# Six tiles for the broadcasts of B and C, three for the weight pieces, five for the convolutions' results, in a decoder layer on one core

## The chip, the cores and the metric

The kernel runs on one core of one Trainium2 chip. The core has five engines that run side by side: PE (matrix products), DVE (vector work), ACT (activation functions and copies), POOL (here small fills and copies, and the DMAs with indices) and SP, which only issues DMAs. Each takes its instructions in its own fixed order and waits at semaphores for the others. On-chip memory (SBUF) has 128 partitions; PE writes into a small second memory (PSUM).

The metric is the device time of one execution in microseconds. The kernel before takes 5619.11 us, the median of three runs (5616.44 to 5622.24).

## What is computed

Input x is 8 x 512 x 512, with a context of the same size. Three parts follow each other, each added to its input and normalised over the last axis (all float32):

```python
x = _layernorm(x + mamba(x))              # L0_attn: state-space layer
x = _layernorm(x + cross_attn(x, ctx))    # L0_xattn: 16 heads of 32, softmax over 512 keys
x = _layernorm(x + moe(x))                # L0_ffn: 32 experts, 4 per token, and a shared one
```

The first part is what the change is in:

```python
xn = layernorm(x) * ln_w + ln_b
x_main, z = split(xn @ in_proj_w, 2)                 # 1024 channels each
x_main = silu(causal_conv(x_main, conv_w) + conv_b)  # 4 taps, per channel
dt, B, C = split(x_main @ x_proj_w, [32, 48])        # 32 | 16 states | 16 states
dt = softplus(dt @ dt_proj_w + dt_proj_b)
h_t = exp(A * dt_t) * h_{t-1} + dt_t * B_t * x_t     # per channel and state
y_t = sum_n h_t * C_t
out = res_scale * ((y + x_main * D) * silu(z)) @ out_proj_w + x
```

The mixture of experts picks 4 of 32 experts per token (first 4 of 8 groups by their best score, then the 4 best scores), gives each expert 640 places, and sends every token's row to its places; the gate's small comparisons are touched by the change too.

## The kernel before

Three functions run after each other: `layers` (state-space layer, attention, gate and shared expert, for all batches), `experts` and `finish` (the last normalisation). All of the change is in `layers`.

`layers` goes through 16 chunks: 8 batches b, each in two halves t of T = 256 tokens. A chunk has 32 steps k = 0 to 31: four channel pairs q, in each four groups g of four states, in each two channel blocks (L980, L1032). A step is, in this order: copy the state into h (`carry`, on ACT), four exponentials for the next step's decays (`decays`, L437, ACT), then on DVE the product of dt*x and B (L449) and the scan over 256 tokens (L453), then the product with C (L470), and on PE the sum over states into `py` (L474). The tile h has four buffers, the decays two.

Beside the steps run, at fixed k, the parts of the same and of neighbouring chunks:

- k = 1, 2: `back`, the out-projection of the chunk before (L503), then its norm and the store to x1d;
- k = 3 to 6: `gate_x`, the z half of the in-projection (L305);
- k % 8 = 3: `prepare` of the next channel pair: dt by one small matmul, on ACT Abs, Relu, Exp, Ln (L406, tile `l`) and Identity (L408), on DVE four operations (L412 to L415; `l` is read last at L414), and eight loads that lay dt and dt*x out as `both` (L426);
- k = 5, 9, 11: load, norm and transpose of the next chunk's x;
- k = 12, 15, 18, 21: `convolve` for the next chunk: in-projection (L305), POOL puts the tail of the last chunk in front (L322, L324), ACT copies PSUM behind it (L325, tile `xp`) and makes the first tap (L331, tile `xs`), DVE adds three taps (L339);
- k = 23, 24: silu and `x_proj` for the next chunk, whose B and C go to DRAM (`scr`).

Side work, the attention, gate and shared expert of batch b - 1, is a list of units with weights, strewn over the steps (L1080); the last batch's runs alone at the end of `layers` (L1102). Then `experts` begins.

Three kinds of loads matter here, all issued by SP (L381, L265, L426). `bcast` (L374) loads the next group's two tiles, B and C, each in two halves, broadcast over 64 partitions: 128 KB written per load, four loads per two steps, from the pool `l_bc` of four tiles. `pieces` (L246) yields the in- and out-projection's weights in pieces of 512 KB, always asked for one piece ahead, in two buffers of the tile `wm`. The convolutions' results `xs` live from the convolution to the end of their channel pair in the next chunk, in six buffers.

A tile pool gives each tag its number of buffers; a new tile of a tag takes the buffer of the oldest and must wait for its last reader. The program text is not the order of issue: a planner in the framework orders each engine's instructions at build time by readiness as it estimates it and by program order, and may draw an instruction far ahead when its inputs and a free buffer are there. On the chip the order is then fixed.

Of the kernel before, what the change touches and what calls it, by code (L numbers as in the profile page):

```python
# [7 lines left out]
F32 = mybir.dt.float32  # L8
# [8 lines left out]
P = 128  # L17
B, S, D = 8, 512, 512
# [8 lines left out]
T = 256  # L27
# [7 lines left out]
SC = S // P  # L35

E = 32
K = 4
G = 8
# [3 lines left out]
CAP = int(1.25 * N * K / E)  # L43
SLOTS = E * CAP
# [37 lines left out]
def layers(ctx, tc, a, x1d, filld, based, xbuf):  # L82
# [23 lines left out]
    nc = tc.nc  # L106
    cp = ctx.enter_context(tc.tile_pool(name="l_const", bufs=1))
    sm = ctx.enter_context(tc.tile_pool(name="l_small", bufs=2))
    gm = ctx.enter_context(tc.tile_pool(name="l_gate", bufs=1))
    p1 = ctx.enter_context(tc.tile_pool(name="l_p1", bufs=1))  # L110
    p2 = ctx.enter_context(tc.tile_pool(name="l_p2", bufs=2))
    p3 = ctx.enter_context(tc.tile_pool(name="l_p3", bufs=2))
    bcp = ctx.enter_context(tc.tile_pool(name="l_bc", bufs=4))
    dp = ctx.enter_context(tc.tile_pool(name="l_dram", bufs=2, space=DRAM))
    psm = ctx.enter_context(tc.tile_pool(name="l_psm", bufs=2, space=PSUM))
    psy = ctx.enter_context(tc.tile_pool(name="l_psy", bufs=1, space=PSUM))
# [14 lines left out]
    def rows(w):  # L131
        return w.rearrange("(c p) f -> p c f", p=P)
# [29 lines left out]
    for da in das:  # L162
# [21 lines left out]
        pattern=[[1, G], [-1, G]],  # L184
        compare_op=ALU.is_gt,
        fill=0.0,
        base=0,
        channel_multiplier=0,
    )

    early = cp.tile([P, SC, E], F32, name="l_early")
    nc.gpsimd.iota(
        early, pattern=[[0, SC], [-1, E]], base=E, channel_multiplier=0, allow_small_or_imprecise_dtypes=True
    )
    first = cp.tile([P, SC, E], F32, name="l_first")
    nc.gpsimd.iota(
        first, pattern=[[0, SC], [CAP, E]], base=-SLOTS, channel_multiplier=0, allow_small_or_imprecise_dtypes=True
    )

    taken = cp.tile([P, SC + 1, E], F32, name="l_taken")  # L200
    nc.gpsimd.memset(taken, 0.0)
# [44 lines left out]
    def pieces():  # L246


        w_in, w_out = rows(a["in_proj_w"]), rows(a["out_proj_w"])
        xs = [w_in[:, :, 2 * q * P : 2 * (q + 1) * P] for q in range(CC // 2)]  # L250
        zs = [w_in[:, :, DI + 2 * q * P : DI + 2 * (q + 1) * P] for q in range(CC // 2)]
        outs = [w_out[:, 2 * q : 2 * q + 2, :] for q in range(CC // 2)]
        n = B * (S // T)
        order = list(xs)
        for i in range(n):
            order += (outs if i else []) + zs + (xs if i + 1 < n else [])
        order += outs
        got = None
        for src in order + [None]:
            nxt = None  # L260
            if src is not None:
                nxt = p2.tile([P, 4 * 2 * P], F32, tag="wm", name="wm").rearrange(
                    "p (c f) -> p c f", c=src.shape[1]
                )
                nc.sync.dma_start(nxt, src)  # L265
            if got is not None:
                yield got
            got = nxt

    piece = pieces()  # L270

    def load_x(b, t, f):
# [27 lines left out]
    def project(f, name):  # L300
        w = next(piece)
        ps = psm.tile([P, 2, T], F32, tag="mm", name=name)
        for i in range(2):
            for dc in range(DC):
                nc.tensor.matmul(  # L305
                    ps[:, i, :],
                    w[:, dc, i * P : (i + 1) * P],
                    f["xnT"][:, dc, :],
                    start=(dc == 0),
                    stop=(dc == DC - 1),  # L310
                )
        return ps

    def convolve(t, q, f):

        c0 = 2 * q
        ps = project(f, "ps_x")

        def first_tap():
            xp = p1.tile([P, 2, T + 3], F32, tag="xp", name="xp")  # L320
            if t == 0:
                nc.gpsimd.memset(xp[:, :, 0:3], 0.0)  # L322
            else:
                nc.gpsimd.tensor_copy(xp[:, :, 0:3], conv_tail[:, c0 : c0 + 2, :])  # L324
            nc.scalar.copy(xp[:, :, 3:], ps)  # L325
            if t < S // T - 1:
                nc.gpsimd.tensor_copy(conv_tail[:, c0 : c0 + 2, :], xp[:, :, T : T + 3])
            f["xs"][q] = xs = p2.tile([P, 2, T], F32, tag="xs", name="xs", bufs=6)
            for i in range(2):
                c = c0 + i  # L330
                nc.scalar.activation(  # L331
                    xs[:, i, :], xp[:, i, 0:T], AF.Identity, bias=cb[:, c : c + 1], scale=cw[:, c, 0:1]
                )

            def other_taps():
                for i in range(2):
                    acc = xs[:, i, :]
                    for k in range(1, 4):
                        nc.vector.scalar_tensor_tensor(  # L339
                            acc, xp[:, i, k : k + T], cw[:, c0 + i, k : k + 1], acc, ALU.mult, ALU.add  # L340
                        )

            return other_taps

        return first_tap
# [28 lines left out]
    def bcast(f, g):  # L374

        got = []
        for r0 in (g * NG, NST + g * NG):
            t = bcp.tile([P, NG // 2, T], F32, tag="bc", name="bc")
            for r in range(2):
                n0 = r0 + r * NG // 2  # L380
                nc.sync.dma_start(  # L381
                    t[r * HP : (r + 1) * HP], f["scr"][n0 : n0 + NG // 2, :].partition_broadcast(HP)
                )
            got.append(t.unsqueeze(1).to_broadcast([P, 2, NG // 2, T]))
        return got

    def prepare(q, f):

        ps = psm.tile([P, 2, T], F32, tag="mm", name="ps_dt")
        for i in range(2):  # L390
            c = 2 * q + i
            nc.tensor.matmul(
                ps[:, i, :], w_dt[:, c * P : (c + 1) * P], f["xd"][0:RANK, :], start=True, stop=True
            )

        def exponentials():
            u = p1.tile([P, 2, T], F32, tag="u", name="u")
            dt = p1.tile([P, 2, T], F32, tag="dt", name="dt")

            for i in range(2):  # L400
                c = 2 * q + i
                nc.scalar.activation(u[:, i, :], ps[:, i, :], AF.Abs, bias=b_dt[:, c : c + 1])
                nc.scalar.activation(dt[:, i, :], ps[:, i, :], AF.Relu, bias=b_dt[:, c : c + 1])
            nc.scalar.activation(u, u, AF.Exp, scale=-1.0)
            l = p1.tile([P, 2, T], F32, tag="l", name="l")
            nc.scalar.activation(l, u, AF.Ln, bias=1.0)  # L406
            w = dtx = p1.tile([P, 2, T], F32, tag="dtx", name="dtx")
            nc.scalar.activation(w, u, AF.Identity, bias=1.0)  # L408

            def both():  # L410

                nc.vector.scalar_tensor_tensor(w, w, -1.0, u, ALU.add, ALU.subtract)  # L412
                nc.vector.tensor_tensor(l, l, w, ALU.subtract)
                nc.vector.tensor_tensor(dt, dt, l, ALU.add)  # L414
                nc.vector.tensor_tensor(dtx, dt, f["xs"][q], ALU.mult)  # L415
                for i in range(2):
                    c = 2 * q + i
                    nc.scalar.activation(
                        f["xs"][q][:, i, :], f["xs"][q][:, i, :], AF.Identity, scale=dpar[:, c : c + 1]
                    )  # L420
                f["ready", q] = []
                for src in (dt, dtx):
                    to = p2.tile([P, 2, 2, T], F32, tag=f"both{len(f['ready', q])}", name="both")
                    for r in range(2):
                        for j in range(2):
                            nc.sync.dma_start(to[r * HP : (r + 1) * HP, :, j, :], src[j * HP : (j + 1) * HP])  # L426
                    f["ready", q].append(to)

            return both

        return exponentials
# [7 lines left out]
    def carry(t, c, g):  # L439

        last = state[:, c, g].unsqueeze(2)
        h = p3.tile([P, NG, T + 1], F32, tag="h", name="h", bufs=4)
        nc.scalar.copy(h[:, :, 0:1], last if t else nothing)  # L443
        return h
# [99 lines left out]
    def choose(b, x2t, pl, st):  # L544
# [13 lines left out]
        square = [P, SC, G, G]  # L558
        other = gs.unsqueeze(2).to_broadcast(square)
        own = gs.unsqueeze(3).to_broadcast(square)  # L560
        eq = gm.tile(square, F32, tag="g_eq", name="g_eq")
        nc.vector.tensor_tensor(eq, other, own, ALU.is_equal)
        nc.vector.tensor_tensor(eq, eq, lower.unsqueeze(1).to_broadcast(square), ALU.mult)
        gt = gm.tile(square, F32, tag="g_gt", name="g_gt")
        nc.vector.tensor_tensor(gt, other, own, ALU.is_gt)
        nc.vector.tensor_tensor(gt, gt, eq, ALU.add)
        nc.vector.tensor_reduce(rank.unsqueeze(3), gt, AX.X, ALU.add)
# [438 lines left out]
    f = {}  # L1006
# [12 lines left out]
    bc, n = bcast(f, 0), 0  # L1019
# [3 lines left out]
    for i, (b, t) in enumerate(chunks):  # L1023
# [8 lines left out]
        for k, (q, g, ci) in enumerate(steps):  # L1032
# [5 lines left out]
            h = carry(t, 2 * q + ci, g)  # L1038
# [57 lines left out]
        f = nf  # L1096
# [322 lines left out]
```

## Time and profile before

| | |
|---|---|
| median of three runs | 5619.11 us (5616.44 to 5622.24) |
| profiled execution | 5620.06 us, its span 5617.3 us |
| granted PE clock, mean | 0.934 |
| layers up to the last scan | about 0 to 3725 us |
| last attention, gate and shared expert | about 3725 to 4000 us |
| experts and last norm | about 4000 to 5617 us |
| loads of bc | 1024, of 128 KB |
| loads of wm | 192, of 512 KB |

In the page and in the answers of the trace a line such as L449 is a line of the kernel; names are tiles, output ahead of the arrow. "Idle before" is the time that an engine stood still ahead of an instruction, and the name behind it what released it. Matmuls are pipelined, so PE's busy time is not PE at its peak. A DMA is listed with the engine that issues it (SPq), at the time of issue.

### The profile page before, as it was taken

The page shows a single profiled execution, that of the slowest core. Times are in us where ns is not written, and L with a number is a line of the kernel's source. Part 1 is how long each engine was busy: PE and PEld are TensorE (multiplying, and loading weights), DVE is VectorE, ACT ScalarE, POOL GpSimd, SP SyncE. Part 2 cuts the span into 40 slices and gives each one's busy share as a digit, 9 for nine tenths or more (in the row PEclk, how much of TensorE's full clock was granted, in tenths as well). Part 3 has the DMA queues.
Part 4 walks back from the last instruction along what each step waited for, and adds up shares of the span by engine and source line. Part 5 has one row for each costly group of instructions (what it writes and reads, how often), then busy time and mean ns, then how long its engine had stood idle before and what let it go on. Part 6 is the DMA issues. An engine that isn't in the chain of part 4 may idle for free. (4 is left out here: it accounts for less than half of the span.)

```text
span 5617.3 us, 60406 instructions
## 1 busy us (share of the span) xinstructions
PE 4888.6 (87%) x19752; PEld 2725.6 (49%) x19752; DVE 4351.5 (77%) x5738; ACT 2592.2 (46%) x5480; POOL 546.1 (10%) x424
## 2 busy tenths in 40 slices
PE   5667888888888988888888898879899999999994
PEld 3333344434433434443443443333577777777773
DVE  5988888989889998898989899854555655555554
ACT  4454555655556555565545656523122222222223
POOL 0000002001100200200010020010111111111111
PEclk8778999999999999999999999989899999999997
DMA  6777345434534534543463453431444444444444
GB/s 207 215 219 201 99 129 177 128 112 130 189 107 113 190 107 122 177 132 106 124 204 94 125 183 110 115 118 45 137 124 126 124 124 119 125 126 124 120 117 138
DMA packets 560426, 769.83 MB, mean 137 GB/s; under 512 B 135754, under 2 KB 268394, under 8 KB 560112
## 3 DMA queue, kind: packets, MB, share of 16 engines
q1 hardware_dynamic: 522608, 680.70, 40.2%
q0 software_dynamic: 33280, 76.90, 7.0%
q10 hardware_dynamic: 4224, 8.39, 0.4%
q8 instruction: 156, 2.56, 0.2%
q14 instruction: 158, 1.29, 0.1%
HBM read 508.68 MB, written 165.05 MB: 120 GB/s over the span
## 5 line engine op out<-in xcount | busy, mean ns | idle before, releaser
L437 ACT ACTIVATE l_da<-both,l_aneg 128x256 f32<-128x256 f32 x2048 | 888.4, 499 | 801.8 <-DVE h L453 759.7
L453 DVE TENSOR_TENSOR_SCAN h<-l_da,h 128x1028 f32<-128x1028 f32 x512 | 1171.2, 2295 | 48.5 <-ACT h L443 26.4
L474 PE MATMUL py<-h,l_twice 128*64 128x256 f32 x4096 | 628.1, 420 | 217.4 <-DVE h L470 217.3
L449 DVE TENSOR_TENSOR h<-both,bc 128x1024 f32<-128x1024 f32 x512 | 619.2, 1216 | 97.2 <-PE py L474 45.4
L470 DVE TENSOR_TENSOR h<-h,bc 128x1024 f32<-128x1024 f32 x512 | 623.5, 1220 | 6.0
L474 PEld LDWEIGHTS py<-h,l_twice 128*64 128x64 f32 x4096 | 295.3, 147 | 587.6 <-DVE h L470 260.7
L766 PE MATMUL ps_s<-l_ka,l_qa 64*128 64x512 f32 x1024 | 317.1, 699 | 142.9 <-DVE mx L768 142.7
L1199 PE MATMUL ps_h<-xT,w 128*128 128x320 f32 x1536 | 435.6, 433 | 0.0
L1279 POOL DMA_INDIRECT based<-y,xe x160 | 250.5, 1565 | 1317.2 <-ACT y L1302 579.9
L768 DVE TENSOR_REDUCE mx<-ps_s 128x2 f32<-128x1024 f32 x256 | 310.8, 1217 | 83.7 <-PE ps_s L766 82.9
L1220 DVE TENSOR_TENSOR hT<-ps_h,p 128x320 f32<-128x320 f32 x128 | 62.9, 492 | 374.7 <-PE ps_h L1199 374.6
L1199 PEld LDWEIGHTS ps_h<-xT,w 128*128 128x128 f32 x1536 | 292.4, 191 | 118.4 <-issue 0.8
L792 PE MATMUL ps_t<-l_qa,l_ka 64*128 64x512 f32 x1024 | 302.0, 654 | 15.8 <-ACT eT L796 11.9
L796 ACT ACTIVATE eT<-ps_t 128x1024 f32<-128x1024 f32 x256 | 259.1, 1013 | 111.9 <-PE ps_t L792 111.5
L808 PE MATMUL po<-eT,l_va 128*64 128x512 f32 x1024 | 279.2, 623 | 23.0 <-ACT raw L820 19.0
L1199 PE MATMUL ps_h<-t,s 128*128 128x320 f32 x1024 | 286.1, 432 | 0.0
L641 POOL DMA_INDIRECT xbuf<-x2t,dest x128 | 216.7, 1693 | 622.1 <-DVE dest L635 583.7
L305 PE MATMUL ps_z<-xnT,wm 128*128 128x256 f32 x1024 | 246.3, 395 | 31.2 <-DMA wm<-in_in_proj_w 28.4
L503 PE MATMUL po<-wm,zs 128*128 128x512 f32 x512 | 246.7, 634 | 13.0 <-DMA wm<-in_out_proj_w 8.5
L703 PE MATMUL ps_p<-x2T,wa 128*128 128x512 f32 x512 | 244.7, 627 | 11.1 <-DVE hT L883 9.1
L305 PE MATMUL ps_x<-xnT,wm 128*128 128x256 f32 x1024 | 245.3, 393 | 1.4 <-ACT xnT L294 1.1
L305 PEld LDWEIGHTS ps_z<-xnT,wm 128*128 128x128 f32 x1024 | 196.2, 196 | 83.7 <-ACT l_da L437 27.1
(225 smaller groups left out, 7397.0 us busy)
## 6 DMA issues: line engine op xcount, KB each, us to landing
bc<-scr SPq DMA_DIRECT2D x1024, 128.0 KB
w<-in_w SPq DMA_DIRECT2D x96, 1024.0 KB
wm<-in_in_proj_w SPq DMA_DIRECT2D x128, 512.0 KB
xbuf<-zero SPq DMA_DIRECT2D x32, 1362.5 KB
xe<-xbuf SPq DMA_DIRECT2D x32, 1362.5 KB
both<-dt SPq DMA_DIRECT2D x256, 128.0 KB
both<-dtx SPq DMA_DIRECT2D x256, 128.0 KB
wm<-in_out_proj_w SPq DMA_DIRECT2D x64, 512.0 KB
```

Source lines behind the costliest of these rows:

```text
L305: nc.tensor.matmul(ps[:, i, :], w[:, dc, i * P : (i + 1) * P], f["xnT"][:, dc, :], start=(dc == 0), stop=(dc == DC - 1),)
L437: nc.scalar.activation(da[:, n, 1:], dt[:, c % 2, j, :], AF.Exp, scale=aneg[:, c, j, g, m : m + 1])
L449: nc.vector.tensor_tensor(steps, dtx[:, c % 2].unsqueeze(2).to_broadcast([P, 2, NG // 2, T]), bc[0], ALU.mult)
L453: nc.vector.tensor_tensor_scan(flat, da.rearrange("p n t -> p (n t)"), flat, 0.0, ALU.mult, ALU.add)
L470: nc.vector.tensor_tensor(steps, steps, bc[1], ALU.mult)
L474: nc.tensor.matmul(py[j * HP : (j + 1) * HP, c % 2, :], twice, h[:, j * 2 + m, 1:], start=False, stop=(s == (NST // NG - 1, NG // 2 - 1, 1)),)
L766: nc.tensor.matmul(ps[:, j, :], qa[r, lt * P : (lt + 1) * P], ka[r, :], start=True, stop=True)
L768: return lambda: nc.vector.tensor_reduce(mx[:, lt, :].unsqueeze(2), ps, AX.X, ALU.max) and None
L792: nc.tensor.matmul(ps[:, j, :], ka[r, kc * P : (kc + 1) * P], qa[r, :], start=True, stop=True)
L796: nc.scalar.activation(eT, ps, AF.Exp)
L808: nc.tensor.matmul(po[j * 2 * HD : (j + 1) * 2 * HD, :], va[:, kc, i, j * HD : (j + 2) * HD], eT[:, j, :], start=(kc == 0), stop=(kc == SC ...
L1199: nc.tensor.matmul(ps, w[:, n, r * P : (r + 1) * P], x[:, n, :], start=not more and n == 0, stop=n == 1, skip_group_check=more,)
```

## The change

- The pool for the broadcasts of B and C has six tiles in place of four.
- The weight pieces `wm` have three buffers in place of two. The generator still asks for one piece ahead.
- The convolutions' results `xs` have five buffers in place of six.
- The logarithm `l` of `prepare` has no tile of its own any more: it takes the buffer of `xp`, of which there is one.
- The constants `early` and `first` are kept once per partition (32 numbers) and read four times with a stride of zero, where they were kept four times.
- The gate's masks `eq` and `gt` are the two halves of one tile of the tag `row` (two buffers, which values, keys, maxima and others take in turn), where each had its own.

Per partition this adds 4096 bytes for bc and 4096 for wm, and gives back 2048 (xs), 2048 (l), 768 (early, first) and 2048 (masks).

```diff
-    bcp = ctx.enter_context(tc.tile_pool(name="l_bc", bufs=4))
+    bcp = ctx.enter_context(tc.tile_pool(name="l_bc", bufs=6))
...
-    early = cp.tile([P, SC, E], F32, name="l_early")
-    nc.gpsimd.iota(
-        early, pattern=[[0, SC], [-1, E]], base=E, channel_multiplier=0, allow_small_or_imprecise_dtypes=True
-    )
...
+    early = cp.tile([P, E], F32, name="l_early")
+    nc.gpsimd.iota(early, pattern=[[-1, E]], base=E, channel_multiplier=0, allow_small_or_imprecise_dtypes=True)
+    early = early.unsqueeze(1).to_broadcast([P, SC, E])
...
-                nxt = p2.tile([P, 4 * 2 * P], F32, tag="wm", name="wm").rearrange(
+                nxt = p2.tile([P, 4 * 2 * P], F32, tag="wm", name="wm", bufs=3).rearrange(
...
-            f["xs"][q] = xs = p2.tile([P, 2, T], F32, tag="xs", name="xs", bufs=6)
+            f["xs"][q] = xs = p2.tile([P, 2, T], F32, tag="xs", name="xs", bufs=5)
...
-            l = p1.tile([P, 2, T], F32, tag="l", name="l")
+            l = p1.tile([P, 2, T + 3], F32, tag="xp", name="l")[:, :, 0:T]
...
-        eq = gm.tile(square, F32, tag="g_eq", name="g_eq")
+        both = p3.tile([P, D], F32, tag="row", name="g_eq").rearrange("p (n j g h) -> p n j g h", n=2, j=SC, g=G)
+        eq, gt = both[:, 0], both[:, 1]
...
-        gt = gm.tile(square, F32, tag="g_gt", name="g_gt")
```

`first` is changed as `early` is.

More of the change, by code (lines that the diff above doesn't have):

```diff
@@ L189, in layers @@
     )
-    early = cp.tile([P, SC, E], F32, name="l_early")
-    nc.gpsimd.iota(
-        early, pattern=[[0, SC], [-1, E]], base=E, channel_multiplier=0, allow_small_or_imprecise_dtypes=True
-    )
[L195 to L198, printed above, removed]
+    early = cp.tile([P, E], F32, name="l_early")
+    nc.gpsimd.iota(early, pattern=[[-1, E]], base=E, channel_multiplier=0, allow_small_or_imprecise_dtypes=True)
+    early = early.unsqueeze(1).to_broadcast([P, SC, E])
+    first = cp.tile([P, E], F32, name="l_first")
+    nc.gpsimd.iota(first, pattern=[[CAP, E]], base=-SLOTS, channel_multiplier=0, allow_small_or_imprecise_dtypes=True)
+    first = first.unsqueeze(1).to_broadcast([P, SC, E])
     taken = cp.tile([P, SC + 1, E], F32, name="l_taken")
```

## The prediction

> **What bounds the kernel now.** I read the page's busy times first, then the busy times by stretch, the groups of instructions on DVE, SP's own waits, and the time line at the places that these name. Busy shares of the whole span mislead, because two stages lie behind each other:
>
> ```profile
> PE 4888.6 (87%) x19752; PEld 2725.6 (49%) x19752; DVE 4351.5 (77%) x5738; ACT 2592.2 (46%) x5480; POOL 546.1 (10%) x424
> ```
>
> ```profile
> 935.00:3725.00 2790.00, 2431.74 (x9949) 1154.22 (x9947) 2522.46 (x2909) 1576.79 (x3323) 208.22 (x160) 0.94 0.46 136
> 3725.00:4090.00 365.00, 308.50 (x1064) 150.07 (x1065) 150.48 (x287) 89.88 (x138) 39.78 (x40) 0.91 0.32 103
> 4090.00:5617.00 1527.00, 1449.26 (x5930) 1070.81 (x5928) 878.08 (x1640) 429.16 (x926) 242.68 (x155) 0.98 0.48 124
> ```
>
> The columns are PE, PEld, DVE, ACT and POOL busy, the granted clock, the DMA share and GB/s. In the steady part of the layers DVE is busy 2522 of 2790 us, 90%; ACT has 57% and DMA 46%. From 3725 to 4090 the last batch's attention runs alone, on PE. After that come the experts, PE at 95%, which the change does not touch. So an edit is worth something only where it fills one of DVE's gaps before 3725, or shortens the chain between 3725 and 4090. The gaps of DVE's commonest instructions:
>
> ```profile
> L453 DVE TENSOR_TENSOR_SCAN h<-l_da,h 128x1028 f32<-128x1028 f32 x512 | 1171.2, 2295 | 48.5 <-ACT h L443 26.4 <-ACT l_da L437 6.4
> L449 DVE TENSOR_TENSOR h<-both,bc 128x1024 f32<-128x1024 f32 x512 | 619.2, 1216 | 97.2 <-PE py L474 45.4 <-DMA both<-dtx 26.8 <-DMA bc<-scr 11.2
> L339 DVE SCALAR_TENSOR_TENSOR xs<-xp,l_cw,xs 128x256 f32<-128x256 f32 x384 | 164.9, 480 | 46.0 <-ACT xs L331 44.5
> ```
>
> The last column is DVE's idle time ahead of the group and what ended it. The product of step and B (L449) waited for a broadcast (bc) 11.2 us in all, in three places, and 8.9 of these are the very first broadcast, at 81.85 us, which finds its tile free anyway. What the four tiles cost shows on SP, the queue that issues the loads (each row: who waited for whom, us, times, longest):
>
> ```profile
> SPq L381 <- DVE h L449: 286.4, 126, 7.7
> SPq L381 <- DVE h L470: 284.7, 133, 8.9
> ...
> SPq L265 <- PE po L503: 143.2, 60, 12.2
> ...
> SPq L265 <- PE ps_z L305: 59.2, 22, 4.3
> ```
>
> SP stands still 571 us for tiles of bc and 202 us for tiles of wm, and all that is queued behind stands with it. But that is SP's time, not DVE's: in the steady part the first load of a broadcast is issued mostly 9 to 30 us before the first product that reads it. Who really waited for a weight piece:
>
> ```profile
> who waited for it (us, times):
>   PE ps_z L305: 28.4, 12
>   PEld po L503: 9.3, 1
>   PE po L503: 8.5, 1
> ```
>
> **The change part by part.** The sum is made against the profiled execution, 5620.06 us (span 5617.3 and 2.8 around it), 0.95 us over the median of 5619.11.
>
> *Third tile for wm, end of the layers.* One place lies on the path for certain. When the last scan is over, the last out-projection runs alone on PE:
>
> ```profile
> 3742.70 7.03 PE L503 MATMUL po<-wm,zs 128*128 128x512 f32 x16
> ...
> 3746.32 3.82 SPq L265 DMA_DIRECT2D wm<-in_out_proj_w  x2
> ...
> 3758.25 9.69 PE L503 MATMUL po<-wm,zs 128*128 128x512 f32 x16 [8.52 <-DMA wm<-in_out_proj_w]
> ...
> 3766.26 0.75 DVE L512 SCALAR_TENSOR_TENSOR o<-po,l_rs,o 128x512 f32<-128x512 f32 x1 [22.67 <-PE po L503]
> ```
>
> Pieces three and four are asked for when PE has let go of pieces one and two, and PE waits 8.52 us; DVE's norm, the store, the reload and the last attention stand behind it. With a third tile, piece three has been in SBUF long since, and only piece four waits, for the release at 3746.3. Piece three covers 3.5 us of PE from 3749.7, to 3753.2. Elsewhere a lone piece took 3.6 us from issue to use (1443.77 to 1447.59, two issues), so piece four is there. The 16 matmuls right behind the pause also took 9.69 instead of 7.03 us. Gain between 0 (the four stores and 16 scattered rows in flight hold piece four up) and 8.5 + 2.7 = 11.2. I take 10, near the upper end, since half the bytes fall out of the window.
>
> *Third tile for wm, elsewhere.* Of the 28.4 us before ps_z, six waits of 3 to 6 us make 24.5 (977, 1447, 1918, 2389, 2862 and 3333 us). At 1447.59 DVE has two products and two scans ahead of it, 6.8 us, and PE catches up under them. I take 0; the cover gone, all 28.4 would have been on the path, so 0 to -28.
>
> *Six tiles for bc.* No instruction is added or taken away: 1024 loads of 128 KB before and after. DVE's waits that have a slot wait of SP directly ahead are bc without the first, 2.3 us, and the reload of x1 (xr) behind bc in the queue, 6.0 us before L449 and 2.4 before L856: 10.7. The waits for both (dtx), 26.8, mostly begin with DVE's own L414 and eight issues of 0.65 us, not with a slot. Bounds 0 and -37.5; I take -7, two thirds of 10.7, because a wait of DVE that goes lets the next one, for PE or ACT, come up.
>
> *Five tiles for xs.* The fifth-last tile's last reader (L462, a matmul) ended more than 12 us before each of the writes (L331), so no write would wait: 0, and no gain either.
>
> *One slot for l and xp.* This adds waits. In program order, l of the third preparation comes between the third and fourth convolution: ACT's logarithm (L406) may not start before DVE's last tap (L339).
>
> ```profile
> 1311.79 2.04 DVE L339 SCALAR_TENSOR_TENSOR xs<-xp,l_cw,xs 128x256 f32<-128x256 f32 x5
> ...
> 1313.33 0.63 ACT L406 ACTIVATE l<-u 128x512 f32<-128x512 f32 x1
> ```
>
> Here L406 begins 0.50 us before the taps end. Behind it on ACT stand L408, the next copy into h and the decays; for these DVE waits. Such overlaps: 0.5 us or so in seven later chunks (3.7 us in all), and larger ones in the first two, 131.86 to 141.26 (9.4, xp behind l), 164.02 to 185.50 (21.5) and 365.03 to 373.67 (8.6). In the first of these DVE came to the preparation only at 187.69, after the taps in any case. ACT idles 3.9 us before most decays (L437 waited 759.7 us for scans), which covers 0.5. POOL's copy of the tail into xp, until now made long ahead, also goes behind l's last reader (L414); the copy of ps_x came 2.3 us or more after that outside the first chunks. Bounds 0 and +43.2; I take +1, near the steady rows.
>
> *Constants and g_eq/g_gt.* L585 and L588 read early with a stride of zero: 287 and 291 ns now, and L582, which already reads such an operand, 291: at most 0.004 us x 32 = 0.1 us. The two 256-wide masks become halves of a row tile; its neighbours in that rotation (raw and r before, z behind) are tens of us away. 0.
>
> Sum: -10 + 0 - 7 + 0 + 1 + 0 = -16, 5604 in the profiled execution and 5603 as a median.
>
> *What the sum cannot see.* The order on every engine is made by a planner at build time, out of program order, and it looks for free tiles. Freed tiles and the new slot give it another problem. Its steady pattern is regular: the first product of a batch starts at 1387.6, 1858.7, 2329.7 and 2800.7, each time 471.1 us on, and the extremes of such steps were 470.2 and 473.9. A change of pattern as large as that spread, 3.7 us over seven batches, is 26 us, of either sign.
>
> **The rivals.** *Larger gain.* Each chunk has 19 to 26 us of DVE gaps, a good part of them at its start, where SP is filled with weight pieces, both and xt. If the planner uses the third piece to draw the out-projection and the gates together, the waits for both (26.8), the steady part of those for xt (42.0 less 5.6 and 9.5 at the first two chunks, 26.9) and the six of 3.6 us for L408 (22) shrink: 76 us at most, half of it 38, so 5565 with the sum above. For it: pieces were issued within 0.03 us of PE's release in chunk after chunk. Against it: xt waits for the store of x1d, which no tile here touches. The Trainium skill, Perfetto Trace Analysis, section Optimization Strategy, reads a gap that repeats on the engine that should be saturated as possibly too few buffers for the next tile. By that rule taken whole, this is the case; the trace bears it out for SP alone, as DVE's gaps end mostly with PE and ACT.
>
> *No change.* The gain of 16 is eaten by the shared slot: only the 21.5 at 164 us, put on ACT's queue ahead of decays, is enough: 5603 + 21.5 = 5624 if all of it lands on the path, 5619 with three quarters. It decides as soon as DVE finds a scan waiting for ACT there. Against it: DVE had work of its own to 187.69.
>
> *Slower: loads issued earlier stand ahead of both.* SP issues in order. With more tiles free, pieces of 512 KB and broadcasts go out at once, and the eight loads of both, for which DVE waits within 3 us, come behind them. Place: the start of each of 15 chunks, and the price is one piece's 3.6 us: 54 us, less 16, is 5657. It decides when a piece's load lands between L414 and both, where now a slot wait holds it back. For it: 1438.37 to 1443.66, both issued in one run with the piece just behind. Against it: no bytes are added and SP has 46% DMA share. The Trainium skill, DMA: Bandwidth & Descriptors, section Queues, rings and completion order, says that descriptors of one queue are taken in ring order, which would make a bulk load ahead of a small one cost just that; no run here shows two orders of the same loads yet. A planner that comes out 3.7 us a batch worse (+26 - 16, 5629) falls on this side too.
>
> **How the numbers follow.** What tells from no change here is about 0.2%, 11 us. The forecast (gains of 3 to 30 us, 5590 to 5608) has 0.34, the larger gain (5535 to 5590) 0.15, no change 0.17, slower 0.34, since another order is as likely to be worse. Faster 0.49, same 0.17, slower 0.34. The likeliest is 5603, its own range 5590 to 5612. The range over the cases leaves out the lowest third of the larger gain (0.05) and the top of the slower case (0.1): 5545 to 5662.
>
> **What would show it.** Right: PE's wait before the second half of the last L503 falls from 8.5 to below 1 us, and x16 takes 7.0 us there; SP's waits at L381 for L449 and L470 and at L265 fall from 773 us to under 200; L449's wait for bc keeps the 8.9 of the start; L406 begins at the end of L339 where it now begins 0.5 us before it; the batch stays at 471 us; the experts stay at 1527 us. Wrong: the distance from batch to batch moves by more than 2 us, whichever way; waits for both grow past 26.8 us; L453 waits for ACT more than 33 us; or the gap before the first expert's transposes, 22 us of waiting for its rows, moves because tiles lie elsewhere in SBUF.

## The result, and the profile after

| | before | after |
|---|---|---|
| median | 5619.11 us (5614.95 to 5622.24, 5 runs) | 5591.35 us (5577.88 to 5593.43, 5 runs) |
| ratio | | 0.9946, 95% interval 0.9932 to 0.9960 |
| profiled execution, its span | 5620.06, 5617.26 us | 5591.35, 5589.48 us |
| end of the last scan | 3724.26 us | 3706.40 us |
| from there to the issue of the last store of x1d | 48.7 us | 39.4 us |
| from there to the end | 1844.3 us | 1843.6 us |

The change gains 27.8 us, 0.54%. Up to the last scan 17.9 us went, in the last out-projection 9.3, behind it 0.6. Lines of `kernel.py` behind L200 have numbers lower by two from here on (L449 of before is L447 of after, and so on); kernels made from the one before keep its numbers.

The busy times by stretch of the kernel after, in the columns that the prediction named:

```profile
935.00:3706.00 2771.00, 2415.45 (x9947) 1142.20 (x9945) 2515.79 (x2904) 1574.38 (x3320) 217.84 (x161) 0.94 0.48 137
...
4062.00:5589.00 1527.00, 1449.28 (x5930) 1070.60 (x5928) 877.06 (x1640) 428.40 (x926) 243.48 (x155) 0.98 0.49 124
```

The work is the same and DVE is still at 91% of the steady part (2515.79 of 2771); in the last 1527 us, the experts, PE is busy for 1449.3 us in both kernels. So what went is idle time of DVE: between the first and the last scan 340.6 us before and 327.1 after, with 3.4 us less busy time; the first scan also begins 1.0 us earlier. Which idle time it was, by DVE's groups of the kernel after (busy, mean ns, and what ended the idle time ahead):

```profile
L447 DVE TENSOR_TENSOR h<-both,bc 128x1024 f32<-128x1024 f32 x512 | 617.7, 1214 | 142.8 <-PE py L472 79.3 <-DMA both<-dtx 36.3 <-DMA bc<-scr 13.4
...
L410 DVE SCALAR_TENSOR_TENSOR dtx<-dtx,u 128x512 f32<-128x512 f32 x64 | 43.3, 677 | 12.7 <-ACT dtx L406 12.7
...
L73 DVE BATCH_NORM_STATS2 st<-xt 128x6 f32<-128x512 f32 x32 | 20.6, 682 | 18.6 <-DMA xt<-in_x 18.6
```

Two of these groups, which the prediction did not show, stood like this before:

```profile
L412 DVE SCALAR_TENSOR_TENSOR dtx<-dtx,u 128x512 f32<-128x512 f32 x64 | 43.6, 682 | 37.1 <-ACT dtx L408 37.1
...
L73 DVE BATCH_NORM_STATS2 st<-xt 128x6 f32<-128x512 f32 x32 | 20.7, 685 | 42.0 <-DMA xt<-in_x 42.0
```

The waits that shrank are those for ACT's L408 (37.1 to 12.7) and for the input of the next chunk (xt, 42.0 to 18.6). The wait of L447, which the six tiles were to shorten, grew from 97.2 to 142.8, its part for bc among it (11.2 to 13.4).

SP's own waits (who waited for whom, us, times, longest):

```profile
SPq L379 <- DVE h L468: 242.2, 127, 5.1
...
SPq L379 <- DVE h L447: 217.1, 105, 7.7
```

With L263 for PE (114.5 and 47.8 us) SP still stands 622 us for tiles of bc and wm in these four rows, 773 before, although it asks for them further ahead. Of the waits for a piece of wm, PE's 28.4 us before ps_z are gone, and 1.7 us before po are left. The end of the layers, from the time line:

```profile
3724.90 10.46 PE L501 MATMUL po<-wm,zs 128*128 128x512 f32 x24
3728.53 0.38 SPq L263 DMA_DIRECT2D wm<-in_out_proj_w  x1
...
3737.11 3.70 PE L501 MATMUL po<-wm,zs 128*128 128x512 f32 x8 [1.75 <-DMA wm<-in_out_proj_w]
```

Three pieces run without a pause, 24 matmuls in 10.46 us; the fourth was asked for at 3728.53 and first used 8.6 us later.

**Where the 17.9 us before went.** From chunk 3 on (counted from 0), two chunks, that is one batch, took 470.7 to 472.9 us before, mean 471.4, and after 464.4 to 470.4, mean 467.8. Six times 3.6 is 21.7 us; the first chunks and the last gave back 4. Both halves of a batch became shorter: counted from first scan to first scan, the six first halves (chunks 4, 6 and so on to 14) lost 12.0 us together and the six second halves (chunks 3 to 13) 9.9. What changed in the first halves shows in chunk 6 (counted from 0), from the time lines; first before (its first scan starts at 1390.94):

```profile
1405.62 3.80 SPq L265 DMA_DIRECT2D wm<-in_out_proj_w  x2
...
1409.43 1.90 PE L474 MATMUL py<-h,l_twice 128*64 128x256 f32 x16
1413.47 1.08 PE L474 MATMUL py<-h,l_twice 128*64 128x256 f32 x6 [2.13 <-DVE h L470]
1414.48 7.13 PE L503 MATMUL po<-wm,zs 128*128 128x512 f32 x16
...
1436.20 0.69 DVE L412 SCALAR_TENSOR_TENSOR dtx<-dtx,u 128x512 f32<-128x512 f32 x1 [3.63 <-ACT dtx L408]
...
1442.59 1.29 DVE L73 BATCH_NORM_STATS2 st<-xt 128x6 f32<-128x512 f32 x2 [3.51 <-DMA xt<-in_x]
```

and then after (first scan at 1386.28):

```profile
1404.76 1.03 PE L472 MATMUL py<-h,l_twice 128*64 128x256 f32 x8
1405.73 7.13 PE L501 MATMUL po<-wm,zs 128*128 128x512 f32 x16
...
1428.33 0.68 DVE L410 SCALAR_TENSOR_TENSOR dtx<-dtx,u 128x512 f32<-128x512 f32 x1
1434.19 1.28 DVE L73 BATCH_NORM_STATS2 st<-xt 128x6 f32<-128x512 f32 x2
```

In PE's queue 22 sums over states (py) stood ahead of the third piece of the out-projection, the last six of them waiting for DVE; now 8 do. The third piece starts 19.4 us behind the chunk's first scan and no longer 23.5, PE's small matmul for the next dt at 33.0 and no longer 36.5, the store of x1d goes out at 39.0 and no longer 43.2, and xt's load, 3 us behind that store, at 41.8 and no longer 46.4. The waits of 3.63 and 3.51 us on DVE are gone. The same happens in chunks 4, 6, 8, 10, 12 and 14: before they hold 21.6 us for L408 and 17.1 for xt, after 0.0 and 0.0. In the second halves of the batches the third piece starts at 35.7 to 38.9 us in both kernels. 38.7 us were gained so, and in the same first halves the waits for PE's py grew by 31.3 us and those for both by 6.4.

In the second halves py's waits fell, from 57.8 to 42.2 us in the six. DVE's waits for py in chunk 5, before:

```profile
DVE h L449 <- PE py L474: 6.0, 3, 2.9
DVE zs L486 <- PE py L474: 5.0, 2, 4.3
```

and after:

```profile
DVE h L447 <- PE py L472: 3.9, 3, 2.3
...
DVE zs L484 <- PE py L472: 2.1, 1, 2.1
```

The earlier third piece does not account for this: e5, e6 and e7 below have it too, and 53.3 to 55.7 us of py in their second halves. Runs e9 to e11 bear on it. Over the whole stretch from the first scan to the last, the waits for py (85.6 to 105.3 us) and for both (26.8 to 36.3) grew by 29 us, and smaller ones moved by less.

### The profile page after: what moved, and what is told of

Same layout as the page of the kernel before. It is cut to its first block, busy times and chain, and to the rows that moved or that the text cites. A ratio compares the mean times of both kernels' runs of the same rounds, so it can differ in the third digit from the quotient of the medians.

```text
span 5589.5 us, 60354 instructions
## 1 busy us (share of the span) xinstructions
PE 4867.0 (87%) x19752; PEld 2713.8 (49%) x19752; DVE 4347.5 (78%) x5738; ACT 2590.3 (46%) x5481; POOL 558.4 (10%) x424
## 3 DMA queue, kind: packets, MB, share of 16 engines
q1 hardware_dynamic: 522608, 680.70, 41.7%
## 5 line engine op out<-in xcount | busy, mean ns | idle before, releaser
L451 DVE TENSOR_TENSOR_SCAN h<-l_da,h 128x1028 f32<-128x1028 f32 x512 | 1169.7, 2291 | 51.9 <-ACT h L441 29.2
L447 DVE TENSOR_TENSOR h<-both,bc 128x1024 f32<-128x1024 f32 x512 | 617.7, 1214 | 142.8 <-PE py L472 79.3
L501 PE MATMUL po<-wm,zs 128*128 128x512 f32 x512 | 232.9, 604 | 2.2 <-DMA wm<-in_out_proj_w 1.7
L1197 PEld LDWEIGHTS ps_h<-t,s 128*128 128x128 f32 x1024 | 194.6, 190 | 81.1
```

The lines of the kernel that those rows point to most:

```text
L447: nc.vector.tensor_tensor(steps, dtx[:, c % 2].unsqueeze(2).to_broadcast([P, 2, NG // 2, T]), bc[0], ALU.mult)
L451: nc.vector.tensor_tensor_scan(flat, da.rearrange("p n t -> p (n t)"), flat, 0.0, ALU.mult, ALU.add)
L1197: nc.tensor.matmul(ps, w[:, n, r * P : (r + 1) * P], x[:, n, :], start=not more and n == 0, stop=n == 1, skip_group_check=more,)
```

## The experiments

The first four runs asked which edit carries the gain: the third buffer of wm (W), the six tiles of bc (B), or the economies, as xs, l, constants and masks are called here. What they showed led to the theory of the rest (S): either buffer alone is enough for the planner to place the third piece earlier on PE, so that the two are substitutes. Each expectation says what its rivals are; W of e5 is another than W of e1 to e4.

Times of different calls are compared by their ratio to the kernel before on the same chip (its medians were 5616.5 to 5620.5). The last two columns are DVE's idle time between the first and the last scan, summed from the trace: for xt and L408 together, and for py and both together. Each trace is of one execution; those of e7, e5 and e3 took 15, 9 and 5 us more than the kernel's median, so their waits are rather too high.

| kernel | wm | bc | economies | median, us | ratio (95% interval) | xt + L408 | py + both |
|---|---|---|---|---|---|---|---|
| before | 2 | 4 | none | 5619.11 | 1 | 63.4 | 112.4 |
| e10_xs5 | 2 | 4 | xs | 5618.80 | 1.0000 (0.9991 to 1.0009) | 61.8 | 111.2 |
| e9_shared_l | 2 | 4 | l | 5615.82 | 0.9993 (0.9984 to 1.0002) | 61.5 | 100.0 |
| e3_economies | 2 | 4 | all | 5612.40 | 0.9990 (0.9981 to 0.9999) | 63.9 | 102.9 |
| e6_bc6_alone | 2 | 6 | none | 5604.88 | 0.9979 (0.9969 to 0.9988) | 24.3 | 145.6 |
| e2_wm2 | 2 | 6 | all | 5596.46 | 0.9963 (0.9950 to 0.9977) | 25.1 | 135.0 |
| e5_wm3_alone | 3 | 4 | none | 5597.64 | 0.9962 (0.9949 to 0.9976) | 16.7 | 151.5 |
| e11_shared_l_wm3 | 3 | 4 | l | 5586.74 | 0.9950 (0.9937 to 0.9964) | 17.3 | 141.8 |
| e1_bc4 | 3 | 4 | all | 5586.01 | 0.9943 (0.9929 to 0.9957) | 15.2 | 133.9 |
| e7_both_alone | 3 | 6 | none | 5597.41 | 0.9960 (0.9946 to 0.9974) | 16.7 | 158.5 |
| e4_own_l | 3 | 6 | all but l | 5595.29 | 0.9962 (0.9948 to 0.9975) | 16.9 | 146.2 |
| after | 3 | 6 | all | 5591.35 | 0.9946 (0.9932 to 0.9960) | 17.8 | 141.6 |

### e1: the change with four tiles for bc

```diff
-    bcp = ctx.enter_context(tc.tile_pool(name="l_bc", bufs=6))
+    bcp = ctx.enter_context(tc.tile_pool(name="l_bc", bufs=4))
```

> The changed kernel with four tiles for the broadcasts again, all else as changed. DVE's order of instructions is the same as in the changed kernel; SP's differs. Theory W (the third weight piece brings the gain; SP's waits for broadcast tiles never reached DVE): 5591 us plus or minus 4, the last out-projection still 9 us shorter, waits for the start of the x load (xt) still near 12 us. Rival B (six tiles keep SP from standing still, so that what is queued behind comes earlier): the gain before the last scan, 17.9 us, goes, 5609; waits for xt and xr go back up to 36 and 8.

5586.01 us. The six tiles add nothing that can be measured to the third buffer of wm.

### e2: the change with two buffers for wm

```diff
-                nxt = p2.tile([P, 4 * 2 * P], F32, tag="wm", name="wm", bufs=3).rearrange(
+                nxt = p2.tile([P, 4 * 2 * P], F32, tag="wm", name="wm").rearrange(
```

> The changed kernel with two buffers for the weight pieces again, all else as changed. Theory W: nearly all of the gain goes, 5614 to 5622; PE waits 8.5 us again in the last out-projection, the way from the last scan to the store of x1d is 49 us again and not 40, and DVE's waits for xt are back near 36 us. Rival B: only the 9 us at the end go, 5600.

5596.46 us: most of the gain stays, so the third buffer of wm is not nearly all of it. With e1, either buffer can go while the other is there, for all or most of the gain.

### e3: the economies alone

The edits of e1 and e2 together: xs, l, constants and masks as in the change, bc and wm as before.

> Only what gives room back: five tiles for xs, l in the buffer of xp, the constants kept once, the masks in a row tile; four tiles for the broadcasts and two for the weight pieces as before. Theory W: the shared slot costs 0 to 5 us, 5619 to 5624. Rival S (the shared slot puts the planner on another and better order, and the buffers do little): 5600 to 5608. The worst case of the prediction's step on the shared slot would be 5662.

5612.40 us, 0.1% under before, and the interval ends at 0.9999. The economies do not cost anything, and the waits for xt and L408 are those of before:

```profile
L410 DVE SCALAR_TENSOR_TENSOR dtx<-dtx,u 128x512 f32<-128x512 f32 x64 | 43.5, 679 | 38.4 <-ACT dtx L406 38.4
...
L73 DVE BATCH_NORM_STATS2 st<-xt 128x6 f32<-128x512 f32 x32 | 20.7, 685 | 42.7 <-DMA xt<-in_x 42.7
```

### e4: the change with a tile of its own for l

```diff
-            l = p1.tile([P, 2, T + 3], F32, tag="xp", name="l")[:, :, 0:T]
+            l = p1.tile([P, 2, T], F32, tag="l", name="l")
```

> The changed kernel with a tile of its own for l again, all else as changed. Theory W: the shared slot was worth 0 to 5 us against the change, so 5586 to 5591. Rival S: slower, 5600 or more. ACT's logarithm then begins before the end of DVE's taps again in the chunks where it did before.

5595.29 us, ratio 0.9962 where the change has 0.9946, with intervals that overlap. The shared slot does not cost anything.

### e5, e6, e7: each buffer alone, and both, without the economies

```diff
-                nxt = p2.tile([P, 4 * 2 * P], F32, tag="wm", name="wm").rearrange(
+                nxt = p2.tile([P, 4 * 2 * P], F32, tag="wm", name="wm", bufs=3).rearrange(
```

> The kernel before with a third buffer for wm and nothing else (bc stays at four tiles, xs at six, l, the constants and the masks keep tiles of their own). Theory S (substitutes): either buffer alone makes room for the planner to finish the out-projection of the chunk before some 4 us earlier in the first half of each batch; the third piece of it then starts about 19.5 us behind a chunk's first scan where it starts at 23.5, and DVE's waits for L408 (27.0 us in seven places) and most of those for xt (36.4) go. With the tail's 9 to 10 us: 5585 to 5598, like the change itself (5591). Theory W (as predicted: the third wm tile is worth the tail's 10 us alone, the rest needs bc): 5606 to 5612, with the waits for xt and L408 as before. Theory E (the economies made room or a better order, since the run with them alone took 5612): 5600 to 5606.

```diff
-    bcp = ctx.enter_context(tc.tile_pool(name="l_bc", bufs=4))
+    bcp = ctx.enter_context(tc.tile_pool(name="l_bc", bufs=6))
```

> The kernel before with six tiles for bc and nothing else. Theory S: 5596 to 5606; the waits for L408 and xt shrink as with the third wm tile, the tail keeps its 49 us from the last scan to the last store of x1d, and DVE's waits for bc and xr, which the prediction meant to remove (10.7 us), give at most half of what is gained. As predicted (-7 us through bc and xr): 5612, waits for L408 and xt unchanged. Theory E (the gain of six bc tiles with the economies came from the economies' order): 5615 to 5620.

Both edits:

> The kernel before with three buffers for wm and six for bc, without any of the economies. Theory S: the two do not add up, 5583 to 5596, no better than the third wm buffer alone by more than 4 us. If they add up (some 25 us for wm, 15 or more for bc): 5575 to 5580. Theory E (the economies' order is worth the 6 us that they showed alone): 6 us slower than the change, 5597.

5597.64, 5604.88 and 5597.41 us: 0.38%, 0.21% and 0.40%. The two do not add up (S; e5 at the slow end of what S expected, e7 1.4 us beyond it). E falls as a reason for the gain of the buffers (e6: 5615 to 5620 expected); the 6 us that it expected of the economies beside them came in e7, of which more below. In all nine kernels that have either buffer (these, the change, e1, e2, e4, e11 and e12; e8 is told by itself) the waits for xt and L408 are at 15 to 25 us, in the four that have neither at 61 to 64. The six first halves from chunk 4 to 14 take 1338.0 to 1345.1 us together in those nine, and 1350.5 to 1360.0 in those four. How six tiles of bc can do it is to be seen in the time line of e6, at the place shown above:

```profile
1403.82 1.03 PE L474 MATMUL py<-h,l_twice 128*64 128x256 f32 x8
1407.45 7.13 PE L503 MATMUL po<-wm,zs 128*128 128x512 f32 x16 [2.60 <-DMA wm<-in_out_proj_w]
```

PE has the order of the kernel after, 8 sums and then the third piece, although the piece is asked for 14.7 us behind the chunk's first scan, as before. PE now waits 2.60 us for it and even so starts it 1.4 us earlier (1.0 to 3.3 us in the six like chunks). So the piece is not asked for any earlier here; the order on PE is another. It is so in every trace: in these chunks 22 sums stand between the second and the third piece in the four kernels that have neither buffer, and 8 in all others. Why six tiles bring the planner to that order no run shows.

### e8: a fifth buffer for h

The changed kernel with four tiles for bc, and:

```diff
-        h = p3.tile([P, NG, T + 1], F32, tag="h", name="h", bufs=4)
+        h = p3.tile([P, NG, T + 1], F32, tag="h", name="h", bufs=5)
```

> The changed kernel with four tiles for bc again and the room given to a fifth buffer for h. DVE's largest remaining idle time before the last scan is ahead of the product of step and B and of the product with C, where PE's sums over states (py) still read the buffer of h that DVE wants: 91 to 105 us. If the number of h buffers is what holds DVE there, a fifth takes away half of it or more, partly given back to ACT's copies into h and its decays: 5540 to 5570. If PE is late because side work stands ahead of its sums, for longer than one step of DVE (2.2 us), only a quarter goes: 5565 to 5580. If the two decay buffers bind next, the waits for l_da and h by ACT grow by what py loses: 5580 to 5592.

5709.67 us, ratio 1.0163 (1.0149 to 1.0177): slower by 92 us than before and by 124 than e1, so all three expectations failed. DVE's waits of e1:

```profile
DVE h L447 <- PE py L472: 66.2, 28, 5.2
DVE h L447 <- DMA both<-dtx: 43.0, 21, 7.0
...
DVE xs L337 <- ACT xs L329: 36.1, 23, 6.4
```

and of e8:

```profile
DVE h L447 <- DMA both<-dtx: 87.0, 24, 7.9
DVE xs L337 <- ACT xs L329: 78.3, 30, 6.3
...
DVE h L447 <- PE py L472: 28.4, 15, 7.2
```

The wait that the buffer was meant for did shrink: all of py from 90.9 to 41.2 us between the first and the last scan. But both rose by 44, xs by 42, L406 by 29, the attention's ps_s by 28 and ps_p by 29, and the whole idle time from 320.3 to 453.4. The work is the same again (DVE busy 4332 us), in another order. That the planner draws the scans ahead of what prepares them fits this; it was not tested. PE's granted clock from 935 us to the last scan was also lower, 0.92 against 0.94 in e1; what part that has in the time is open.

### e9, e10, e11: parts of the economies

e9 and e11 share l's slot (the reverse of the edit of e4, made on the kernel before), e11 with the edit of e5 besides. e10:

```diff
-            f["xs"][q] = xs = p2.tile([P, 2, T], F32, tag="xs", name="xs", bufs=6)
+            f["xs"][q] = xs = p2.tile([P, 2, T], F32, tag="xs", name="xs", bufs=5)
```

> The kernel before with one edit: the logarithm l takes xp's buffer. All three runs that have the economies lie 6 to 12 us under their twins without them (5612 and 5617 or 5618; 5586 and 5598; 5596 and 5605), and the change with an own l lies 4 over the change. Theory L (the shared slot itself gives this, by another order of DVE and PE; SP's order stays): 5608 to 5613. As predicted (the slot costs about 1): 5618 to 5620. Theory M (the masks in a row tile, or where tiles come to lie, give it): 5616 to 5619.

> The kernel before with one edit: five buffers for xs. The order of the instructions on every engine is that of before, so only the addresses of tiles differ and a wait that never binds is added. As predicted: no change, 5615 to 5620. If the places of tiles matter (theory A): outside 5611 to 5624, of either sign.

> The kernel before with two edits: l in xp's buffer and a third buffer for wm; this is a third of the change's edits and takes 2 KB more than before. Theory L: as fast as the changed kernel with four bc tiles, 5583 to 5592. Theories M and A: like the third wm buffer alone, 5595 to 5600.

e10 is no change. e9 took 5615.82 us, with an interval that holds 1. In each of three pairs that differ in l's slot alone the kernel that shares it is faster, by the ratios 0.07% (e9 and before), 0.12% (e11 and e5) and 0.16% (the change and e4), which is 4 to 9 us, and waits less for py: 64.6 against 85.6, 99.7 against 113.2, 105.3 against 111.9. The traces add two things. On PE, on ACT and among SP's issues e9 has the order of e3, e11 that of e1, and e7 that of e4, instruction for instruction, so of the economies only l's slot reaches these queues. And in the six second halves from chunk 3 to 13 DVE waits for py 37.6 to 47.0 us in the seven kernels that share the slot, and 48.9 to 57.8 in the six that do not (e8 left out). So the 9.9 us that the change gained there fit L. But e1 and e11, with one order on PE, are 9 us apart in that sum, and no pair of intervals is apart: a gain from the slot is likely and not shown. e11 and e1 differ in xs, masks and constants, and take 5586.74 and 5586.01: these three are worth nothing that can be measured.

### e12: a fourth buffer for wm

The changed kernel with four tiles for bc and `bufs=4` for wm.

> The changed kernel with four tiles for bc again and the room given to a fourth buffer for wm. At the end of the layers the fourth piece of the last out-projection then needs no release by PE; with three buffers PE stood 1.6 to 5.3 us for it and the matmuls behind took up to 2.6 us more. Theory T (the tail's loss is the piece's late issue): no wait of PE between the 32 matmuls, 14 us from the first to the last, and the last store of x1d is issued 37.5 us behind the last scan, where three buffers gave 39.2 to 45.5. In the steady part theory S expects nothing more, since the waits for xt and L408 are gone already: 5576 to 5586. If a fourth buffer draws the planner into another order as the fifth h buffer did: 5595 or more.

5594.90 us, ratio 0.9960 (0.9947 to 0.9974). At the end of the layers T holds:

```profile
3734.48 13.90 PE L501 MATMUL po<-wm,zs 128*128 128x512 f32 x32
```

No pause, and the last store of x1d is issued 37.6 us behind the last scan (37.5 expected; e1 39.2). The time is not better than e1's: in the profiles (16.4 us apart, the medians 8.9) the first four chunks take 13.4 us longer than e1's, and the rest up to the last scan 3.4; DVE's waits for xs are 37.0 us where e1 has 27.9. So no kernel tried is measurably faster than the change; e1 and e11 match it with fewer edits.

## Why the prediction was right, and where not

The forecast was 5603 us, faster with 0.49, and 5591.35 lies in its own range of 5590 to 5612. The steps behind it did less well than the number, which is in part luck: the 10 us at the end came as 9.3 in this pair of profiles, the 7 of the six tiles did not come, and 17.9 us came before the last scan, 12.0 of them in the halves where PE's order changed as shown, which the sum had left out.

- **Third tile for wm, end of the layers: -10.** Between the two profiles it is -9.3, PE's wait fell from 8.52 to 1.75 us, and the last sixteen matmuls run without it in 7.3 us. But the pair flatters the step. With two buffers, six kernels (before, e2, e3, e6, e9, e10) have 48.7, 45.5, 48.8, 45.6, 46.1 and 45.1 us from the last scan to the store, mean 46.6; with three, six kernels (after, e1, e4, e5, e7, e11) have 39.4, 39.2, 45.5, 41.3, 45.3 and 39.3, mean 41.7 (e8, with a third buffer and another order throughout, has 47.9). By these means the step is worth some 5 us. What was wrong in it is "so piece four is there": the 3.6 us came from a piece in the steady part (3.8 at the place named) and is the short end of a range, for the pieces that PE waited for in that same profile took 3.6 to 6.3 us there; here it takes 8.4 to 12.1 us from issue to first use, as the lower bound of the step had allowed. e12 shows the rest: without that issue the wait is gone.
- **Third tile for wm, elsewhere: 0.** This failed. Alone it gains about 20 us (e5), 5 of them at the end. The prediction looked at PE's six waits before ps_z, and rightly found cover for them; what counted was how many sums stand ahead of the third piece in PE's queue.
- **Six tiles for bc: -7, through bc and xr.** The sign was right for the edit alone (-12, e6), and the mechanism was not. DVE's waits for bc without the first rose from 2.5 to 8.3 us. Those for xr fell from 8.4 to 3.3, but e10, which has the order of before, also has 3.4: that fall is scatter. On top of the third buffer the tiles give nothing (e1 and after).
- **Five tiles for xs: 0.** Right (e10).
- **One slot for l and xp: +1.** The wait came as described: L404 now waits for the taps, 5.0 us in six places, 1.77 of them near the place of the 21.5 us overlap. It cost nothing that shows. The upper end, +43.2, is refuted by e3, e4 and e9, and the sign is likely wrong too (e9 to e11). The reading that ACT idles 3.9 us before most decays does not hold: in the profile before it stood idle ahead of L437 350 times, 2.3 us in the mean.
- **Constants and masks: 0.** Right as far as e1 and e11 can tell.
- **What the sum cannot see.** This decided. The text named a change of pattern of up to 3.7 us a batch, of either sign; it came as -3.6, about half of it in each half of the batch.
- **The rivals.** "Larger gain" had the mechanism: out-projection and gates drawn together, the waits for xt and L408 shorter. They fell by 45.6 us of 63.4, more than the half it took, but it did not ask what comes up next: both grew where it was to shrink, and with py took 29 back. "No change" through the shared slot fell with e4. "Slower" had both held up by 54 us; both rose by 9.5.
- **The bands.** They do not quite fit the words: 5590 to 5608 are gains of 11 to 29 us, not of 3 to 30, and the lowest third of 5535 to 5590 ends at 5553, not at 5545.
- **What would show it.** PE's wait in the last out-projection was to fall below 1 us and fell to 1.75. SP's waits for wm and bc were to fall under 200 us and stand at 622. A freed buffer is asked for sooner and waits again. It was a poor sign, for e1 stands 719 us in the same rows and shows the gain. Of the four signs of being wrong three came: the batch distance moved by more than 2 us, the waits for both passed 26.8, and the scan's waits for ACT passed 33 (29.2 and 8.1). They told rightly that the steps did not fit; the fourth, the gap before the first expert, stayed at 22 us. L404 begins at the end of the taps, as foretold.

The rule from the Trainium skill (Perfetto Trace Analysis, section Optimization Strategy), that a gap which repeats may mean too few buffers, was given as this change's case. The runs support it by half: the repeated waits for xt and L408 went with one buffer more, of either of two tags that they do not belong to; and in e8 the largest repeated gap shrank with a buffer for the very tile that it waits for, and the kernel lost 1.6%.

## What to carry to other kernels

Where a planner makes the order at build time, a buffer more is first of all another order: find in the trace the place where one engine's queue changes (here 22 or 8 sums ahead of a piece) before any gain is put down to a tile that arrives earlier, and try each buffer alone, since two that both open the same place do not add up. A queue's waits for free tiles say little of what a tile is worth; the idle time of the engine that bounds the stage does, and of what goes there a good part comes back as the next wait (29 of 46 us here). A step read off one place in one profile, like the end of the layers here, is uncertain by the scatter of that place, 45.1 to 48.8 us in six profiles.

## What the runs showed that was not expected

- **The same order scatters.** e10 has the order of before on every engine and its time (ratio 1.0000), and yet in its trace, taken in another call, the last scan ends 4.7 us later (3728.98), single chunks differ by up to 4.6 us, and PE's wait at the end of the layers is 5.59 instead of 8.52 us. One of DVE's groups of e10:

```profile
L449 DVE TENSOR_TENSOR h<-both,bc 128x1024 f32<-128x1024 f32 x512 | 619.4, 1217 | 99.4 <-PE py L474 45.8 <-DMA both<-dtx 29.0 <-DMA bc<-scr 13.9
```

Bc is at 13.9 where before has 11.2. Differences of 2 to 5 us per cause between two profiles are not an effect of an edit.

- **The same load, 512 KB, takes very different times.** From issue to first use, the pieces of wm that PE waited for took 3.6 to 6.3 us in the kernel before, and in the steady part of other kernels 5.9 to 7.8 (the third piece in e6) and 9.0 and 9.4 (once each, e5 and e3). At the end of the layers, where four stores of z and sixteen scattered rows are in flight, it was 8.4 to 12.1. That these hold it up was not tested, and the ranges overlap.
